# Two relational graph attention layers on one core: tail order, first rounds of the second stage, and three early loads of x

## The chip, the cores and the metric

The kernel runs on one NeuronCore of a Trainium2 chip. The core has a matrix engine (TensorE, PE in the profile, with PEld for its weight loads), VectorE (DVE), ScalarE (ACT), GpSimd (POOL) and SyncE (SP), which work in parallel, each through its own instructions in order, and 16 DMA engines. The metric is the device time of one execution in microseconds, as the median of several runs; lower is better.

## The reference

A graph has 3125 nodes with 768 features each and 53125 edges (25000 random pairs in both directions and one loop per node), sorted by destination. Each edge has one of three relations. Two attention layers of this kind follow each other, then a residual and a layer norm:

```
xr = einsum('nd,rdf->rnf', x, W)              # one dense product per relation
oi, oj = xr[etype, dst], xr[etype, src]
alpha = leaky_relu(oi @ q + oj @ k, 0.2)      # per edge and head
a = softmax of alpha over the edges of one destination
out = segment_sum(a * oj, dst) + b
```

Layer 1 has 4 heads of 192 columns, layer 2 one head of 768. Between the layers stands elu; the result is layernorm(x + layer 2(elu(layer 1(x)))). All in float32.

## The kernel before

The nodes are cut into 25 blocks of 128 (`NB`; the last one has 53 rows), the edges into groups that go with the blocks, each of up to `SL` = 17 slots of 128 edges. Every matmul of the dense products is done on a high and a low part of the operands (`wH`, `wL`), so that three products stand for one. Everything is inside a manual schedule: the order in which Python emits instructions is the order on each engine, and events (`ev`, filled through `when`) say at which step `n` or `k` a function is called. There are four stages, with their times in the profiled execution:

- 0 to 122 us: weights are loaded and split, and products of weights with k and q are made.
- `phase1`, 122 to about 995 us: the dense product of layer 1. A step is one `d_group(n)` (block, relation, half of the columns; `po` L698), six steps per block, some 5.8 us each. `d_row` copies the products out (L713) and stores them as rows of a table in memory (`ftab`). Before a block can be multiplied, `x_load` (L500) reads its rows into `xr`, `d_turn` (L670) transposes them on PE (`px`, L675), and `d_split` (L679) cuts them into parts (ACT L682, DVE L683), adds the bias into `share[4]` (L685) and stores that (L686). `xr` is one buffer. `x_next` at step 6b - 7 loads the next block; for blocks 22 to 24 (`GB` = 21) the turn, split and load stand at m = 1, 3, 5, with m = n - 120. A block of fewer than 128 rows is cleared by a memset (L505) before its load. Between these steps run the attention scores of layer 1: SP loads `T`, `w`, `sT` and `q` per block, POOL gathers `kt` (L462) after DVE's `lim` (L557), and so on. `share` is a list of nine row buffers; 0 to 2 take the rows for the table, others the weights of layer 2 while those are cut (`w_load`, `w_split`).
- `phase2`, about 998 to 2000 us: POOL gathers rows of the table, slot by slot `k`; `high` and `sums` work `LAG` = 5 slots behind. DVE compares destinations with a row of numbers and multiplies by the attention (`selp`, L853); PE uses that as weights and adds the rows up (`acc`, L875). The slots of a block are taken in seven `ROUNDS`, and the sums are issued in two `BATCHES` of rounds. Then `e_y` (L883 to L888: divide, add the bias), `e_x` (exp, L894), `e_h` (L898, L899: elu), `e_t` (transposes, L906), `e_s`, `e_s2` (`hT`, L913, L919), the dense product of layer 2 (L931) and its rows (L939). `last_w2` is a generator; each `next` issues one 1152 KB load (L514) of the last relation's weights of layer 2 on ACT's queue, and the fifth one two DVE copies.
- `phase3`, about 2000 to 2735 us: POOL gathers rows `G` of the second table (44 buffers), about 27.4 us per group. DVE and PE make the softmax (`bc` L1033, `oh` L1059, `a_alpha` L1070 and L1075, transposes L1080, `a_scan` L1086 and L1088, `e` L1091, exp L1095, back L1099, `p` L1104). `high` makes `selp` (L1112), from a pool of 10 buffers of 64 columns, two rounds ahead of `sums` (L1126, `acc`). Then come `e_y` (L1158 to L1162), `e_n` (L1169 to L1173: statistics), `e_sd` (the root, ACT L1177), `e_low` (L1189, L1191) and `e_out` (ACT Identity L1196 and the store). Each store has a manual dependency on the one before; the last one is POOL's scatter L1198.

For each group the events of `phase3` are placed by its first slot; the last groups, which have no gathers left behind them, run one after the other.

Of the kernel before, what the change touches and what calls it, by code (L numbers as in the profile page):

```python
# [8 lines left out]
F32 = mybir.dt.float32  # L9
# [11 lines left out]
P = 128  # L21
# [33 lines left out]
def kernel(  # L55
# [442 lines left out]
        s["q"] = work.tile([P, H1 * R * 3], BF, name="q1", bufs=2)  # L498
        nc.sync.dma_start(s["q"], nodes(b, q1_d))

    def x_load(pre, b):
        n = min(P, N - b * P)
        xs[b] = pre.tile([P, D], F32, name="xr", bufs=1)
        if n < P:
            V.memset(xs[b], 0.0)  # L505
        nc.sync.dma_start(xs[b][:n], x[b * P:b * P + n, :])
# [13 lines left out]
    def phase1(pre, work, psum, wH, wL, qq):  # L520
# [270 lines left out]
        ev[6 * NB - 10].append((lambda b: a_last(), 0))  # L791
        for b in range(2, GB + 1):
            for d, f, o in ((-8, d_turn, 0), (-7, d_split, 0), (-7, x_next, 1)):
                ev.setdefault(6 * b + d, []).append((f, b + o))
        for n in range(max(ev) + 1):
            for f, b in ev.get(n, ()):
                f(b)
            b, i = divmod(n, 6)
            if n == 2:
                nc.sync.dma_start(share[3][:, :D], x[:P, :])  # L800
            if n == 8:
                V.tensor_add(share[4][:, :D], share[3][:, :D], b2r)
                nc.sync.dma_start(xb_d[:P, :], share[4][:, :D])
            m = n - 6 * (GB - 1)
            if m in (1, 3, 5):
                d_turn(GB + 1 + m // 2)
                d_split(GB + 1 + m // 2)
                if m < 5:
                    x_load(pre, GB + 2 + m // 2)
            if m in (9, 17):  # L810
                w2s = second_weights(m // 16, wH, wL)
            if 9 <= m < 25:
                next(w2s, None)
            if 2 <= b < 2 + R * DT:
                if i == 0:
                    w_load(b - 2)
                if i == 2:
                    w_split(b - 2)
            if n < len(groups):
                d_group(n, *groups[n])  # L820
            if 0 < n <= len(groups):
                d_row(*groups[n - 1])


    def phase2(work, psum, wH, wL):
# [31 lines left out]
        def sums(k):  # L857

            b, j = in_turn(k)
            n = [i for i, r in enumerate(rounds(b)) if r[-1] == j]  # L860
            batch = [x for x in BATCHES if n and n[0] == x[-1]]
            if not batch:
                return
            if batch[0][0] == 0:
                blk[b] = {"acc": psum.tile([P, 2, 512], F32, name="acc", bufs=2)}
            acc = blk[b]["acc"]
            o = [(i, t) for r in rounds(b) for i in r for t in WINDOW[i]]
            for m, h in ((m, h) for m in batch[0] for h in range(H1)):
                c = slice(h % 2 * CW, (h % 2 + 1) * CW)
                for i, t in o:  # L870
                    if i not in rounds(b)[m]:
                        continue
                    u = [x for x, y in o if y == t]
                    sel, g = st[b, i]
                    T.matmul(acc[32 * t:32 * t + 32, h // 2, c], sel[:, h, 32 * (t - WINDOW[i][0]):][:, :32],  # L875
                             g[:, h * CW:(h + 1) * CW], start=(i == u[0] and h % 2 == 0), stop=(i == u[-1]),
                             skip_group_check=True)

        def e_y(b):
            s = blk[b]  # L880
            acc = s["acc"][:, :, :HW].rearrange("p c (h f) -> p c h f", h=2)
            rz = work.tile([P, 2, 2], F32, name="rz", bufs=2)
            V.tensor_scalar(rz, acc[:, :, :, F1], EPS, None, op0=ALU.add)  # L883
            V.reciprocal(rz, rz)
            y = s["y"] = work.tile([P, D], F32, name="y", bufs=1)
            for h in range(H1):
                f = slice(h * F1, (h + 1) * F1)
                V.scalar_tensor_tensor(y[:, f], acc[:, h // 2, h % 2, :F1], rz[:, h // 2, h % 2:h % 2 + 1],  # L888
                                       bias1[:, f], op0=ALU.mult, op1=ALU.add)

        def e_x(b):
            s = blk[b]
            s["ey"] = work.tile([P, D], F32, name="ey", bufs=1)
            S.activation(s["ey"], s["y"], AF.Exp)  # L894

        def e_h(b):
            s = blk[b]
# [56 lines left out]

        LAG = 5
        first = SLF + LAG - 1
        for d, f in ((0, e_h), (3, e_t), (3, e_s), (3, e_s2)):
            when(first + d, f, order[0])
        for i, b in enumerate(order):
            e = SLF + i * SL + LAG  # L960
# [11 lines left out]
        for k in range(max(ev) + 1):  # L972
            if k < NK:
                gather(k)
            if k in (14, 19, 23, 26, 28):
                next(last_w2, None)
            if 0 <= k - LAG < NK:
                sums(k - LAG)
            if k == first:
                e_y(order[0])  # L980
                e_x(order[0])
            if 0 <= k - LAG + 2 < NK:
                high(k - LAG + 2)
            for f, a in ev.get(k, []):
                f(*a)
            if k == NK + LAG:
                for b in range(len(xbs)):
                    x_load3(b)
# [6 lines left out]
    def phase3(work, psum):  # L995
# [110 lines left out]
        def high(b, n):  # L1106

            for j in rounds(b)[n]:
                p = blk[b]["p"][:, j:j + 1]
                lo, hi = WINDOW[j][0] * 32, WINDOW[j][-1] * 32 + 32  # L1110
                sel = work.tile([P, 64], F32, name="selp", bufs=10)[:, :hi - lo]
                V.tensor_scalar(sel, row_p[:, lo:hi], dl[:, b, j:j + 1], p, op0=ALU.is_equal, op1=ALU.mult)  # L1112
                st[b, j] = sel

# [96 lines left out]
        def when(k, f, *a):  # L1211
            ev.setdefault(k, []).append((f, a))

        LAG = SL + 10
        for b in range(NB):
            when(max(base(b) - 12, 0), a_load, b)
            q = base(b) - 4 if b > 1 else 2 + 12 * b
            for i in range(5):
                when(q + 2 * i, a_spread, b, i)
                when(q + 1 + 2 * i, a_spread2, b, i)  # L1220
            for d, f in ((10, a_q), (11, a_q2), (12, a_q3)):
                when(q + d, f, b)
            e = base(b) + slots(b)
            for d, f in ((2, a_alpha), (3, a_turn), (4, a_scan), (5, a_exp), (6, a_back), (7, a_put)):
                when(e + d, f, b)
            s = base(b) + LAG + max(slots(b) - SL, -1)
            for n in range(len(ROUNDS)):
                when(s + n - 2, high, b, n)
                when(s + n, sums, b, n)
            s += len(ROUNDS)  # L1230
            if b + len(xbs) < NB:
                when(s + 30, x_load3, b + len(xbs))

            for d, f in ((0, e_y), (1, e_n), (4, e_sd), (5, e_low), (7, e_out)):
                when(s + d + (2 if b == NB - 2 and d > 1 else 0), f, b)
        when(base(NB - 1) + SL, e_ready)
        for k in range(max(ev) + 1):
            if k < NK:
# [591 lines left out]
```

## Time and profile before

| | |
|---|---|
| runs of the kernel | 2748.60, 2750.47, 2752.66 us; median 2750.47 us |
| profiled execution | 2741.27 us |
| its span | 2739.5 us |
| its mean TensorE clock | 0.834 of full speed |
| PE busy | 2054.5 us, 75% of the span |
| DVE busy | 1195.6 us, 44% |
| POOL busy | 1322.5 us, 48% |
| ACT busy | 369.7 us, 13% |

All trace times are from the one profiled execution, counted from the span's start; between it and the median of the runs lie 0.33%. Busy shares are averages over four stages with different limits, so windows of one stage say more than the page's sums. A line of a window holds its start and end, its length, then busy time and count of PE, PEld, DVE, ACT and POOL, the granted clock of TensorE, the busy share of the DMA engines, and GB/s. A line of the chain is: start, length, and what the chain spent it on.

### The profile page before, as it was taken

To read this page: it belongs to the slowest core of one execution; us is meant where nothing else is said; L and a number is where in the kernel's file an instruction comes from. 1 tells how busy PE (TensorE), PEld (TensorE's weight loads), DVE (VectorE), ACT (ScalarE), POOL (GpSimd) and SP (SyncE) were. 2 spreads that over 40 slices of the span, in tenths; PEclk is the share of its full clock that TensorE was granted. 3 is DMA by queue.
4 is the path that set the end of the run, shared out by engine and by line. 5 is a ranking of instruction groups with operands and counts; after the bars stand their busy time and mean duration, and the time that the engine had idled before them with its cause. 6 is when DMAs were issued, how large, how long until landed. Compare 5 with 4: busy or idle time off the path is not lost.

```text
span 2739.5 us, 41906 instructions
## 1 busy us (share of the span) xinstructions
PE 2054.5 (75%) x15027; PEld 1606.6 (59%) x15027; DVE 1195.6 (44%) x4159; ACT 369.7 (13%) x658; POOL 1322.5 (48%) x1326
## 2 busy tenths in 40 slices
PE   7867888777776767888888898889936566565655
PEld 6756676667665645777677777767723232333323
DVE  6423333333332245445544554455424545444444
ACT  5301111111111000101110111111100111111111
POOL 3355555454543454444444434443255656566561
PEclk9967888888887878999999999999966777676777
DMA  7533333333332467666665656665577888877781
GB/s 193 142 95 120 114 114 114 113 106 115 103 108 99 143 213 244 198 201 203 203 200 187 214 185 211 192 212 191 175 271 246 272 267 267 276 253 259 251 262 61
DMA packets 156844, 506.31 MB, mean 185 GB/s; under 512 B 43875, under 2 KB 57069, under 8 KB 156628
## 3 DMA queue, kind: packets, MB, share of 16 engines
q0 software_dynamic: 81904, 331.52, 39.8%
q1 hardware_dynamic: 62926, 156.02, 16.1%
q10 hardware_dynamic: 11798, 16.00, 1.9%
q8 instruction: 122, 2.00, 0.3%
q14 instruction: 94, 0.77, 0.1%
HBM read 412.55 MB, written 95.69 MB: 186 GB/s over the span
## 4 chain that ended last, share of the span: by engine, by line
PE 52%; issue 17%; another core or an unknown queue 12%; DVE 11%; POOL 3%; DMA 3%; ACT 1%; POOLq 0%; ACTq 0%; DVEq 0%; SPq 0%
PE po L931 15%; PE po L698 14%; PE acc L875 9%; PE acc L1126 8%; DVE selp L853 3%; POOL G L462 2%; DMA G<-ftab,ridx 1%; PE bank L285 1%; DVE y L888 1%; PE bc L1033 1%; PE pt L263 1%; PE pt L906 1%; PE po L395 1%; DVE selp L1112 1%
## 5 line engine op out<-in xcount | busy, mean ns | idle before, releaser
L462 POOL DMA_INDIRECT kt<-kt,ridx x374 | 393.6, 1052 | 387.7 <-DVE lim L557 266.3
L698 PE MATMUL po<-wH,xT 128*128 128x384 f32 x1584 | 498.5, 382 | 107.5 <-issue 67.0
L931 PE MATMUL po<-wH,hT 128*128 128x386 f32 (+1 forms) x1800 | 514.7, 361 | 31.7 <-issue 27.3
L462 POOL DMA_INDIRECT G<-ftab,ridx x374 | 372.9, 997 | 242.2 <-PE acc L1126 110.4
L1126 PE MATMUL acc<-G,selp 128*32 128x386 f32 x2488 | 343.2, 621 | 102.6 <-DVE selp L1112 79.9
L698 PEld LDWEIGHTS po<-wH,xT 128*128 128x128 f32 x1584 | 331.2, 215 | 145.0 <-issue 92.0
L931 PEld LDWEIGHTS po<-wH,hT 128*128 128x128 f32 x1800 | 353.0, 202 | 67.3 <-issue 61.9
L853 DVE TENSOR_SCALAR selp<-frow,fdl,pall 128x32 f32<-128x32 f32 (+1 forms) x1688 | 380.3, 309 | 20.1 <-remote 17.3
L462 POOL DMA_INDIRECT share<-ftab,ridx x239 | 238.4, 997 | 299.7 <-PE acc L875 223.4
L931 PE MATMUL po<-wL,hT 128*128 128x386 f32 (+1 forms) x900 | 321.9, 358 | 14.4 <-issue 14.4
L698 PE MATMUL po<-wL,xT 128*128 128x384 f32 x792 | 296.2, 374 | 36.3 <-issue 35.8
L1126 PEld LDWEIGHTS acc<-G,selp 128*32 128x32 f32 x2488 | 190.6, 132 | 217.4 <-DVE selp L1112 107.0
L875 PE MATMUL acc<-share,selp 128*32 128x193 f32 x3208 | 229.6, 335 | 35.0 <-issue 31.4
L462 POOL DMA_INDIRECT g<-ftab,ridx x135 | 134.7, 998 | 191.9 <-PE acc L875 146.5
L698 PEld LDWEIGHTS po<-wL,xT 128*128 128x128 f32 x792 | 170.3, 215 | 48.3 <-issue 48.1
L875 PEld LDWEIGHTS acc<-share,selp 128*32 128x32 f32 x3208 | 131.0, 111 | 107.7 <-issue 77.5
L931 PEld LDWEIGHTS po<-wL,hT 128*128 128x128 f32 x900 | 182.4, 203 | 17.7 <-issue 17.4
L939 ACT COPY r<-po 128x386 f32<-128x386 f32 (+1 forms) x150 | 72.2, 481 | 834.5 <-PE po L931 621.4
L875 PE MATMUL acc<-g,selp 128*32 128x193 f32 x1768 | 139.4, 332 | 18.6 <-issue 15.7
L713 ACT COPY share<-po 128x384 f32<-128x384 f32 x144 | 67.1, 478 | 594.3 <-remote 260.6
L943 DVE COPY q<-po 128x1 f32<-128x1 f32 x75 | 11.6, 155 | 275.8 <-ACT r L939 275.7
L1039 DVE TENSOR_SCALAR sT<-bc,cols 128x512 bf16<-128x512 f32 (+1 forms) x125 | 83.4, 668 | 108.1 <-PE bc L1033 87.4
(245 smaller groups left out, 1986.0 us busy)
## 6 DMA issues: line engine op xcount, KB each, us to landing
ftab<-share SPq DMA_DIRECT2D x75, 386.0 KB
ftab<-r SPq DMA_DIRECT2D x75, 386.0 KB
share<-in_L_gnn_W_dram SPq DMA_DIRECT2D x36, 384.0 KB
w_d<-w2hl SPq DMA_DIRECT2D x18, 768.0 KB
sT<-dr_d SPq DMA_DIRECT2D x25, 544.0 KB
share<-in_x_dram SPq DMA_DIRECT2D x25, 384.0 KB
xb_d<-share SPq DMA_DIRECT2D x25, 384.0 KB
xr<-in_x_dram SPq DMA_DIRECT2D x23, 384.0 KB
```

The source lines that it names most:

```text
L263: T.transpose(pt[:, f, c * P:(c + 1) * P], a[:, (2 * i + f) * P:(2 * i + f + 1) * P], ident)
L285: T.matmul(to, a[:, 2 * i + f, :], t[:, f, :w], start=(n == 0), stop=(n == 2 * DT - 1))
L395: T.matmul(po[g][:, :HALF], a[:, t % 2, :], w[:, r * DT + t, c * HALF:(c + 1) * HALF], start=(t == 0 and n == 0), stop=(t == DT - 1 and n ...
L462: return G.indirect_dma_start(out=to, out_offset=None, in_=tab, in_offset=_index(i[:, j:j + 1]), bounds_check=NP * R - 1, oob_is_err=False)
L698: m = T.matmul(po[:, :HALF], xT[:, s, t, :], w[:, i, sl], start=(n == 0), stop=(n == 3 * DT - 1))
L713: S.copy(to, po[:, :HALF].rearrange("p (h f) -> p h f", h=2))
L853: V.tensor_scalar(sel[:, h, :hi - lo], row[:, lo:hi], dl[:, b, j:j + 1], pall[:, b, j, h:h + 1], op0=ALU.is_equal, op1=ALU.mult)
L875: T.matmul(acc[32 * t:32 * t + 32, h // 2, c], sel[:, h, 32 * (t - WINDOW[i][0]):][:, :32], g[:, h * CW:(h + 1) * CW], start=(i == u[0] an ...
L931: T.matmul(po[:, :wd], hT[:, k, t, :], w[:, r * DT + t, sl], start=(t == 0 and n == 0), stop=(t == DT - 1 and n == 2))
L939: S.copy(o[:, c * HW:c * HW + wd], po[:, :wd])
L1039: V.tensor_scalar(s["sT"][:, 4 * i * P:4 * i * P + n], bc[:, :n], cols[:, b:b + 1], None, op0=ALU.is_equal)
L1126: T.matmul(acc[32 * t:32 * t + 32, c, :HW], st[b, j][:, 32 * (t - WINDOW[j][0]):][:, :32], gs[:, (base(b) + j) % NG, c * HW:(c + 1) * HW], ...
```

## The change

- In `phase1`, block 22 of x is loaded into `share[6]` at m = -8 and block 23 into `share[3]` at m = -3; `share[3]` is last read by a weight split at the step before. Block 24 goes into `xr` at the event that used to load block 22 (n = 119). Turn and split stay at m = 1, 3, 5.
- In `phase2`, the sums of block 0 are called round by round and not in two batches. `e_first` takes the place of `e_y`, `e_x` and `e_h` for block 0: exp is done in two halves, the first as soon as two of the four heads are divided, and elu by halves as well, right after. The first of the five calls of `last_w2` moves from slot 14 to 20 (19, 20, 23, 26, 28 in all).
- In `phase3`, `selp` has two tags, 9 buffers of 32 columns and 8 of 64, which is one group's 17. The sums of group 23 (`NB - 2`) move to `NK` + 4 (rounds 0 and 1) and `NK` + 7 (the rest), NK = 422 being the number of slots, and its `e_*` to `NK` + 14 and on. In the emitted order PE's transposes for the softmax of group 24 (L1080) now stand before the sums of group 23, its back transpose (L1099) between rounds 1 and 2 of these, and the sums of group 24 straight behind. DVE has the 17 selps of group 23, then the softmax of group 24, 15 of its selps, `e_y` of 23, two selps, `e_n` of 23, `e_y` and `e_n` of 24, and only then `e_low` of 23 and of 24.

```diff
--- before.py
+++ after.py
@@ -498,9 +498,9 @@
         s["q"] = work.tile([P, H1 * R * 3], BF, name="q1", bufs=2)
         nc.sync.dma_start(s["q"], nodes(b, q1_d))
 
-    def x_load(pre, b):
+    def x_load(pre, b, to=None):
         n = min(P, N - b * P)
-        xs[b] = pre.tile([P, D], F32, name="xr", bufs=1)
+        xs[b] = pre.tile([P, D], F32, name="xr", bufs=1) if to is None else to[:, :D]
         if n < P:
             V.memset(xs[b], 0.0)
         nc.sync.dma_start(xs[b][:n], x[b * P:b * P + n, :])
@@ -791,7 +791,7 @@
         ev[6 * NB - 10].append((lambda b: a_last(), 0))
         for b in range(2, GB + 1):
             for d, f, o in ((-8, d_turn, 0), (-7, d_split, 0), (-7, x_next, 1)):
-                ev.setdefault(6 * b + d, []).append((f, b + o))
+                ev.setdefault(6 * b + d, []).append((f, NB - 1 if f is x_next and b == GB else b + o))
         for n in range(max(ev) + 1):
             for f, b in ev.get(n, ()):
                 f(b)
@@ -805,8 +805,9 @@
             if m in (1, 3, 5):
                 d_turn(GB + 1 + m // 2)
                 d_split(GB + 1 + m // 2)
-                if m < 5:
-                    x_load(pre, GB + 2 + m // 2)
+
+            if m in (-8, -3):
+                x_load(pre, GB + 1 + (m + 8) // 5, share[6 if m == -8 else 3])
             if m in (9, 17):
                 w2s = second_weights(m // 16, wH, wL)
             if 9 <= m < 25:
@@ -858,7 +859,7 @@
 
             b, j = in_turn(k)
             n = [i for i, r in enumerate(rounds(b)) if r[-1] == j]
-            batch = [x for x in BATCHES if n and n[0] == x[-1]]
+            batch = [x for x in (BATCHES if b else [[m] for m in range(len(ROUNDS))]) if n and n[0] == x[-1]]
             if not batch:
                 return
             if batch[0][0] == 0:
@@ -893,6 +894,27 @@
             s["ey"] = work.tile([P, D], F32, name="ey", bufs=1)
             S.activation(s["ey"], s["y"], AF.Exp)
 
+        def e_first(b):
+
+            s = blk[b]
+            acc = s["acc"][:, :, :HW].rearrange("p c (h f) -> p c h f", h=2)
+            rz = work.tile([P, 2, 2], F32, name="rz", bufs=2)
+            V.tensor_scalar(rz, acc[:, :, :, F1], EPS, None, op0=ALU.add)
+            V.reciprocal(rz, rz)
+            y = work.tile([P, D], F32, name="y", bufs=1)
+            ey = s["ey"] = work.tile([P, D], F32, name="ey", bufs=1)
+            for h in range(H1):
+                f = slice(h * F1, (h + 1) * F1)
+                V.scalar_tensor_tensor(y[:, f], acc[:, h // 2, h % 2, :F1], rz[:, h // 2, h % 2:h % 2 + 1],
+                                       bias1[:, f], op0=ALU.mult, op1=ALU.add)
+                if h % 2:
+                    f = slice(h // 2 * HALF, (h // 2 + 1) * HALF)
+                    S.activation(ey[:, f], y[:, f], AF.Exp)
+            for c in range(2):
+                f = slice(c * HALF, (c + 1) * HALF)
+                V.tensor_scalar(ey[:, f], ey[:, f], 1.0, -1.0, op0=ALU.min, op1=ALU.add)
+                V.scalar_tensor_tensor(ey[:, f], y[:, f], 0.0, ey[:, f], op0=ALU.max, op1=ALU.add)
+
         def e_h(b):
             s = blk[b]
             V.tensor_scalar(s["ey"], s["ey"], 1.0, -1.0, op0=ALU.min, op1=ALU.add)
@@ -954,7 +976,7 @@
 
         LAG = 5
         first = SLF + LAG - 1
-        for d, f in ((0, e_h), (3, e_t), (3, e_s), (3, e_s2)):
+        for d, f in ((3, e_t), (3, e_s), (3, e_s2)):
             when(first + d, f, order[0])
         for i, b in enumerate(order):
             e = SLF + i * SL + LAG
@@ -972,13 +994,12 @@
         for k in range(max(ev) + 1):
             if k < NK:
                 gather(k)
-            if k in (14, 19, 23, 26, 28):
+            if k in (19, 20, 23, 26, 28):
                 next(last_w2, None)
             if 0 <= k - LAG < NK:
                 sums(k - LAG)
             if k == first:
-                e_y(order[0])
-                e_x(order[0])
+                e_first(order[0])
             if 0 <= k - LAG + 2 < NK:
                 high(k - LAG + 2)
             for f, a in ev.get(k, []):
@@ -1108,7 +1129,7 @@
             for j in rounds(b)[n]:
                 p = blk[b]["p"][:, j:j + 1]
                 lo, hi = WINDOW[j][0] * 32, WINDOW[j][-1] * 32 + 32
-                sel = work.tile([P, 64], F32, name="selp", bufs=10)[:, :hi - lo]
+                sel = work.tile([P, hi - lo], F32, name=f"selp{hi - lo}", bufs=9 if hi - lo == 32 else 8)
                 V.tensor_scalar(sel, row_p[:, lo:hi], dl[:, b, j:j + 1], p, op0=ALU.is_equal, op1=ALU.mult)
                 st[b, j] = sel
 
@@ -1226,13 +1247,15 @@
             s = base(b) + LAG + max(slots(b) - SL, -1)
             for n in range(len(ROUNDS)):
                 when(s + n - 2, high, b, n)
-                when(s + n, sums, b, n)
+
+                when(s + n if b != NB - 2 else NK + (4 if n < 2 else 7), sums, b, n)
             s += len(ROUNDS)
             if b + len(xbs) < NB:
                 when(s + 30, x_load3, b + len(xbs))
-
+            if b == NB - 2:
+                s = NK + 14
             for d, f in ((0, e_y), (1, e_n), (4, e_sd), (5, e_low), (7, e_out)):
-                when(s + d + (2 if b == NB - 2 and d > 1 else 0), f, b)
+                when(s + d, f, b)
         when(base(NB - 1) + SL, e_ready)
         for k in range(max(ev) + 1):
             if k < NK:
```

## The prediction

> **What bounds the kernel now.** I read the page's chain and engine parts first, then the windows, and the chain and timeline only where a window stood out.
>
> ```profile
> PE 2054.5 (75%) x15027; PEld 1606.6 (59%) x15027; DVE 1195.6 (44%) x4159; ACT 369.7 (13%) x658; POOL 1322.5 (48%) x1326
> PE 52%; issue 17%; another core or an unknown queue 12%; DVE 11%; POOL 3%; DMA 3%; ACT 1%; POOLq 0%; ACTq 0%; DVEq 0%; SPq 0%
> ```
>
> TensorE is the busiest engine and half of the chain. DMA is 3% of the chain, so one exposed load can only be a place, not a bound. The seven windows of the dense stage that run from one block's kt gathers to the next's show such a place. The columns are PE, PEld, DVE, ACT, POOL, granted clock, DMA share and GB/s:
>
> ```profile
> 705.15:740.36 35.21, 27.39 (x142) 23.67 (x141) 11.79 (x34) 4.61 (x9) 17.84 (x18) 0.81 0.34 111
> 740.36:776.52 36.16, 28.58 (x142) 25.12 (x141) 11.78 (x34) 4.51 (x9) 17.78 (x17) 0.76 0.35 108
> 776.52:811.16 34.64, 25.70 (x142) 22.64 (x141) 11.86 (x34) 4.41 (x9) 17.82 (x17) 0.85 0.35 113
> 811.16:847.12 35.96, 27.21 (x142) 23.89 (x141) 11.84 (x34) 4.41 (x9) 17.82 (x18) 0.81 0.31 98
> 847.12:890.19 43.07, 28.41 (x154) 25.78 (x153) 13.27 (x34) 5.08 (x10) 17.88 (x17) 0.76 0.26 86
> ```
>
> The fifth is 7 to 8 us longer than the others at almost the same PE work. The chain of waits inside it, and the windows around the hole, say why:
>
> ```profile
> 873.99 0.67 DVE xr L505
> 874.72 8.62 DMA xr<-in_x_dram
> 883.47 1.52 PE px L675 x6
> ```
>
> ```profile
> 878.00:883.50 5.50, 0.03 (x1) 0.06 (x1) 0.00 (x0) 0.00 (x0) 0.00 (x0) 0.68 0.06 26
> 883.50:887.00 3.50, 3.50 (x14) 3.50 (x15) 1.14 (x2) 1.18 (x2) 0.00 (x0) 0.53 0.00 2
> 887.00:890.20 3.20, 3.20 (x19) 2.89 (x18) 1.54 (x7) 0.00 (x0) 0.01 (x1) 1.00 0.32 125
> ```
>
> The load of block 24 (53 rows) cannot start until block 23 has been split out of the only xr buffer. It takes 8.62 us, PE stands still for 5.50 us of it, and every engine's row is empty. The 3.5 us after that run at a clock of 0.53, 14 PE records where the next 3.2 us hold 19. The tail (timeline of PE) is the second place:
>
> ```profile
> 2694.51 11.76 PE L1126 MATMUL acc<-G,selp 128*32 128x386 f32 x100
> 2709.98 0.80 PE L1080 MATMUL pa<-fident,al 128*17 128x128 f32 x3 [3.71 <-DVE al L1075]
> 2713.24 0.28 PE L1099 MATMUL pa<-fident,e 17*128 17x17 f32 x1 [2.46 <-ACT e L1095]
> 2715.58 11.47 PE L1126 MATMUL acc<-G,selp 128*32 128x386 f32 x100 [2.05 <-DVE selp L1112]
> ```
>
> PE sums group 23, then waits three times for the softmax of group 24, then sums group 24.
>
> **Part 1, the x loads.** Blocks 22 and 23 are read into two idle row buffers many groups ahead, and block 24 into xr as soon as block 21 is out of it, four dense groups (some 23 us) earlier. The 8.62 us load is then hidden by those groups. What goes is the 5.50 us hole and the slow start after it: 14 records at 3.50/14 = 0.250 us against 3.20/19 = 0.168 us is 1.14 us. Sum 6.6 us. The least is 5.5 (wait alone); the most is 43.07 less the shortest undisturbed window, 34.64, so 8.4. From there to the end every engine's order is fixed and POOL's next gathers wait for DVE's lim (L557), 20.3 us in this window, so the shift is carried on. The moved memset (0.67 us on DVE) lies earlier beside dense work, worth nothing now that no load waits for it. On SP the three loads now stand ahead of the row stores and the loads of T, w, sT and q of later blocks. Those are used four or more groups after they are issued, so 0, and one group's 5.8 us if that cover were gone.
>
> The row on the clock is followed by a page that sizes it otherwise. The Trainium skill, "TensorE: Matmul & The Clock Gate", Part 1, says that after an idle window of about 3.4 us TensorE gets half its clock until about 3.4 us of work have passed; half speed over 3.5 us would be 1.75 us here and the sum 7.3, where the rows give 1.14 and 6.6.
>
> **Part 2, the first block of the second stage.** "Singly" moves nothing on PE: built, PE's order in the first block is what it was, because its DVE comparisons already came round by round; 0. What does change is what follows the sums. Before, in the chain:
>
> ```profile
> 1036.56 1.39 DVE y L888 x4
> 1037.95 0.89 DVE selp L853 x4
> 1038.91 0.57 DVE ey L898
> 1039.50 0.97 DVE ey L899
> 1040.52 1.56 PE pt L906 x6
> ```
>
> Now exp of the first half (half of the 0.84 us of L894, by its length) starts when two y are done, about 1037.3, and the four selp come after. The first half's L898 and L899 (0.29 and 0.49) end near 1038.8, the second's near 1039.7. Three transposes (0.78) run from 1038.9, three from 1039.75, so they end at 1040.5, not 1042.07: 1.6 us (bounds 0.9, the selps alone, and 2.0). The four selps serve later sums, which PE reaches after 6.6 us of dense matmuls.
>
> The first 1152 KB load of wH was issued at 1004.47 among the first gathers; it now goes out at about 1038 with three others. In the 50 us window from 990 the DMA engines were 0.77 busy. PE's sums there run 14 us behind the last gather's landing (1022.45 against 1036.13), so the load's absence need not help: I take 0, with up to 4 us of gain (its 1152 KB at the window's 260 GB/s). The other three loads, issued from 1038.06, landed near 1055, so the fourth lands near 1061, and that relation's weights are first read at 1073; 0 again, up to 2 us for block 1's gathers beside it.
>
> **Part 3, selp buffers.** 17 buffers instead of 10 let DVE finish a group's selps without waiting for PE. Those waits are 39.6 us in 47 places, but they end while PE is working through the very sums that release them, and the steady chain is the ping-pong of bc (L1033), softmax and sums. The 99 queue waits of L1112 at 21 ns are 2 us of DVE. I take 0.5 us of gain, from 4 (a tenth of the waits) to a loss of 1.
>
> **Part 4, the tail.** DVE makes all 17 selps of group 23 (0.24 us each from 2694.14: to 2698.3), then a_alpha(24); from sd to pa took 0.8 us, so pa starts near 2699.2 and ends at 2700.0. Then rounds 0 and 1 of group 23 (32 of 100 records) run under scan, exp and all. PE has stood for almost 5 us, so it starts slowly. Rows for that:
>
> ```profile
> 2715.50:2719.00 3.50, 3.42 (x21) 2.84 (x25) 2.73 (x13) 0.65 (x1) 0.00 (x0) 0.50 0.32 119
> 2719.00:2727.00 8.00, 8.00 (x83) 5.83 (x75) 1.35 (x6) 0.00 (x0) 0.00 (x0) 0.95 0.01 3
> ```
>
> Group 23's own first 3.5 us (2694.5 to 2698.0) hold 23 records, 0.152 each; warm it is about 0.10 (83 in 8.0 us here, in 8.3 us there). So 2.7 us hold 18, 14 more take 1.4: 2704.1; e goes back (0.28) to 2704.4; the other 68 take 6.8 to 2711.2; group 24 follows without a gap, warm, 10.0 to 2721.2 instead of 2727.05. That is 5.9 us, but not all of it reaches the end. ACT's Identity of group 23 waits for its low (L1191), which DVE now does behind all of e_n(24): 2721.2 + 2.94 to sd = 2724.15, low and Identity 1.6 more, 2725.7. Its store takes 3.37 us (row of 2716.18), and POOL's last scatter is ordered behind that landing: 0.38 of queue waits, 0.28 to start: 2729.8 against 2732.02, 2.2 us of gain. Bounds: 2.8 at 0.0964 a record; a loss of 0.3 if all 168 later records cost 0.1147 as before.
>
> **Sum.** 6.6 + 1.6 + 0 + 0.5 + 2.2 = 10.9 us. The profiled execution took 2741.27 us (span 2739.5), so 2730.4; it stood 0.33% under the median of the runs, 2750.47, so the median should come to 2739.6. Worst ends together: 5.5 + 0.9 - 2 - 1 - 0.3 = 3.1 of gain, 2747.4; best ends: 8.4 + 2.0 + 4 + 4 + 2.8 = 21.2, 2729.3. A measurement of this kernel tells about 0.2%, 5.5 us.
>
> **Rivals.**
> (a) Given back. The dense stage's recovered time meets another wait: PE idles 7.6 to 8.9 us in every undisturbed window too (7.2 of it for ACT's share, L713), and the stage's last store gates the first gathers (POOL waits 16.5 us for it). If only 5.5 less 3 us survived, with nothing from steady sums and a tail at its loss end, the gain is 2.5 + 1.6 - 0.3 = 3.8: 2746.7, within 0.2%. Against it: PE's idle in the long window is 14.66 us, 6.4 over the others' mean.
> (b) More. The first block's slow sums are the load's doing, and 4 us come back there with 4 in the steady groups: 10.9 + 4 + 3.5 = 18.4, 2732.1. For it: DMA 0.77 busy. Against: PE trails the landings by 14 us.
> (c) Slower. In the last stage DVE's selps, freed of their waits, move to other moments, beside POOL's gather writing (POOL is busy 327 of 540 us from 2080 to 2620) and PE's reads. If this stretches each of 21 steady groups (27.4 us), at 0.78 us a group (2.8%) it costs 16.4 and the result is 5.5 us slower; that is the point from which it decides. At 0.9: 18.9 - 10.9 = 8.0 slower, 2758.5. For it: DVE waits 112.8 us there on something that the trace does not name. Against: the instructions and their order are the same.
> (d) It does not do what it says: rounds singly are already so on PE, and counted at nothing.
>
> **How the numbers follow.** Forecast 0.64, (a) 0.15, (b) 0.10, (c) 0.11; (d) is inside the forecast. Faster by over 0.2%: forecast and (b), 0.74. Within: 0.15. Slower: 0.11. The range reaches up to (a) and the worst ends, and down close to (b): 2731 to 2749.5.
>
> **What would show it.** Right: the long window at 36 us or less, no DMA wait before px; hT of block 0 about 8 us earlier than 1042 in the span (6.6 + 1.6); one cold stretch in the tail and the last scatter bound by the store of group 23. Wrong: px waiting elsewhere, phase-3 groups that are not 27.4 us, PE waiting on wH near 1066 to 1073, or sums of group 24 still at 11.5 us.

## The result, and the profile after

The changed kernel takes 2743.53 us (median of 12 runs), the kernel before 2751.99 us beside it (12 runs). The ratio is 0.9969, with a 95% interval from 0.9955 to 0.9983: 8.5 us faster. The forecast was 10.9 us less, within a range from 2731 to 2749.5 us.

The two profiled executions differ by half a microsecond only (spans of 2739.0 and 2739.5 us). That is no contradiction: single runs spread over 14 to 19 us, and the page of before had caught a run well under its median. In the trace after, the 102nd row copy of the dense stage (L713), up to which both kernels' work is the same, comes at 712.1 us, before at 707.2 us. So stretches are compared below, each between two marks of one profile, and not times from the start.

The dense stage, windows from one block's kt gathers to the next, as in the prediction:

```profile
710.08:744.86 34.78, 26.79 (x142) 23.75 (x141) 11.79 (x34) 4.53 (x9) 17.80 (x18) 0.80 0.36 112
...
815.28:850.58 35.30, 26.95 (x142) 23.58 (x141) 12.48 (x35) 4.61 (x9) 17.73 (x18) 0.81 0.31 102
850.58:887.43 36.85, 27.66 (x154) 24.21 (x153) 12.64 (x33) 5.08 (x10) 17.86 (x18) 0.81 0.26 85
887.43:923.22 35.79, 27.85 (x136) 23.89 (x135) 7.25 (x27) 3.07 (x7) 17.09 (x17) 0.76 0.51 155
```

The window of 43.07 us takes 36.85. PE's timeline shows block 24's transposes without a wait in front, and warm:

```profile
882.28 0.82 PE L675 MATMUL px<-fident,xr 128*128 128x128 f32 x6
```

The first block of the second stage, on DVE before:

```profile
1036.15 0.16 DVE L883 TENSOR_SCALAR rz<-acc 128x4 f32<-128x4 f32 x1 [13.45 <-remote]
...
1040.38 2.63 DVE L853 TENSOR_SCALAR selp<-frow,fdl,pall 128x32 f32<-128x32 f32 x12
1042.93 0.96 DVE L919 TENSOR_TENSOR hT<-pt,hT 128x768 fp32r<-128x768 f32 x1
```

and after, on DVE and on PE:

```profile
1034.96 0.16 DVE L902 TENSOR_SCALAR rz<-acc 128x4 f32<-128x4 f32 x1 [12.07 <-remote]
...
1038.01 0.56 DVE L916 SCALAR_TENSOR_TENSOR ey<-y,ey 128x384 f32<-128x384 f32 x1
1038.48 3.52 DVE L854 TENSOR_SCALAR selp<-frow,fdl,pall 128x64 f32<-128x64 f32 x16
1041.90 0.97 DVE L941 TENSOR_TENSOR hT<-pt,hT 128x768 fp32r<-128x768 f32 x1
```

```profile
1037.76 1.76 PE L928 MATMUL pt<-fident,ey 128*128 128x128 f32 x6 [7.38 <-DVE ey L915]
...
1042.92 1.01 PE L953 MATMUL po<-wH,hT 128*128 128x386 f32 x2 [1.50 <-DVE hT L941]
```

The transposes start 1.6 us earlier against the last sum, as forecast (2.80 us after DVE's rz, before 4.37). But PE then stops for 1.50 us: hT's low part (L941) stands on DVE behind 16 selps and starts 6.9 us after rz, where before (L919) it stood behind 12 and started 6.8 us after. The tail, on PE, ACT and POOL:

```profile
2701.38 0.80 PE L1101 MATMUL pa<-fident,al 128*17 128x128 f32 x3 [4.80 <-DVE al L1096]
2702.11 5.18 PE L1147 MATMUL acc<-G,selp 128*32 128x386 f32 x32
2707.22 0.23 PE L1120 MATMUL pa<-fident,e 17*128 17x17 f32 x1
2707.39 15.79 PE L1147 MATMUL acc<-G,selp 128*32 128x386 f32 x168
```

```profile
2726.49 1.03 ACT L1217 ACTIVATE pall<-pall,low,sd 128x768 f32<-128x768 f32 x1 [7.58 <-DVE low L1212]
...
2728.04 1.03 ACT L1217 ACTIVATE xb<-xb,low,sd 128x768 f32<-128x768 f32 x1 [0.43 <-DVE low L1212]
```

```profile
2731.53 1.02 POOL L1219 DMA_INDIRECT out_dram<-xb,oidx  x1 [43.27 <-issue]
```

PE's 168 last records run in one piece at 0.094 us each. The scatter starts 2.5 us after the end of ACT's last Identity. Before, it was 0.28 us:

```profile
2730.71 1.03 ACT L1196 ACTIVATE xb<-xb,low,sd 128x768 f32<-128x768 f32 x1 [0.43 <-DVE low L1191]
```

```profile
2732.02 1.02 POOL L1198 DMA_INDIRECT out_dram<-xb,oidx  x1 [45.85 <-ACT xb L1196]
```

It now waits for the store of group 23, as the run "Low of group 23 early" below shows.

### The profile page after: what moved, and what is told of

The parts are those of the page before. It is cut to its first block, busy times and chain, and to the rows that moved or that the text cites. A ratio compares the mean times of both kernels' runs of the same rounds, so it can differ in the third digit from the quotient of the medians.

```text
span 2739.0 us, 41794 instructions
## 1 busy us (share of the span) xinstructions
PE 2068.9 (76%) x15027; PEld 1599.4 (58%) x15027; DVE 1190.7 (43%) x4161; ACT 370.0 (14%) x659; POOL 1322.5 (48%) x1326
## 3 DMA queue, kind: packets, MB, share of 16 engines
q0 software_dynamic: 81904, 331.52, 39.9%
## 5 line engine op out<-in xcount | busy, mean ns | idle before, releaser
L698 PE MATMUL po<-wH,xT 128*128 128x384 f32 x1584 | 508.5, 387 | 102.8 <-issue 77.0
L698 PEld LDWEIGHTS po<-wH,xT 128*128 128x128 f32 x1584 | 335.6, 217 | 141.5 <-issue 105.4
L698 PE MATMUL po<-wL,xT 128*128 128x384 f32 x792 | 300.7, 380 | 45.7 <-issue 45.1
L1147 PEld LDWEIGHTS acc<-G,selp 128*32 128x32 f32 x2488 | 179.2, 131 | 225.9 <-DVE selp L1133 117.2
L698 PEld LDWEIGHTS po<-wL,xT 128*128 128x128 f32 x792 | 172.0, 217 | 62.6 <-issue 62.4
L876 PE MATMUL acc<-g,selp 128*32 128x193 f32 x1768 | 138.8, 329 | 17.4 <-issue 16.7
L713 ACT COPY share<-po 128x384 f32<-128x384 f32 x144 | 67.2, 478 | 595.1 <-issue 207.7
```

The source lines that it names most:

```text
L698: m = T.matmul(po[:, :HALF], xT[:, s, t, :], w[:, i, sl], start=(n == 0), stop=(n == 3 * DT - 1))
L713: S.copy(to, po[:, :HALF].rearrange("p (h f) -> p h f", h=2))
L1147: T.matmul(acc[32 * t:32 * t + 32, c, :HW], st[b, j][:, 32 * (t - WINDOW[j][0]):][:, :32], gs[:, (base(b) + j) % NG, c * HW:(c + 1) * HW], ...
```

## The experiments

The runs fell on several chips, and these are not alike. B, C and D are three different chips; which one A was is not on record. Each comparison is made on one chip. The ratio is taken over all runs and is not the quotient of the two medians beside it.

| comparison | before, us | kernel, us | ratio, 95% interval |
|---|---|---|---|
| chip A: the change | 2751.99 | 2743.53 | 0.9969 (0.9955 to 0.9983) |
| chip B: before again | 2054.07 | 2054.06 | 0.9998 (0.9989 to 1.0007) |
| B: x loads alone | 2054.07 | 2051.07 | 0.9986 (0.9977 to 0.9995) |
| B: first block alone | 2054.07 | 2063.18 | 1.0041 (1.0029 to 1.0054) |
| B: tail alone | 2054.07 | 2059.74 | 1.0023 (1.0014 to 1.0033) |
| chip C: the change again | 2685.4 | 2682.68 | 0.9989 (0.9966 to 1.0013) |
| C: low of group 23 early | 2685.4 | 2673.58 | 0.9956 (0.9933 to 0.9980) |
| C: weight load back at slot 14 | 2685.4 | 2677.75 | 0.9972 (0.9949 to 0.9994) |
| C: x loads, halves, hT early | 2685.4 | 2679.76 | 0.9975 (0.9954 to 0.9997) |
| chip D: x loads alone | 2054.92 | 2052.01 | 0.9992 (0.9982 to 1.0001) |
| D: first block alone | 2054.92 | 2065.72 | 1.0051 (1.0038 to 1.0064) |
| D: tail alone | 2054.92 | 2061.53 | 1.0032 (1.0019 to 1.0045) |
| D: mended | 2054.92 | 2060.33 | 1.0027 (1.0016 to 1.0038) |

On B and D the same program takes 700 us less than on A. What is gone there can be read in the waits of the whole run. On A, before, PE, DVE and POOL:

```profile
PE po L698 <- issue: 119.7, 173, 2.4
...
PE acc L875 <- issue: 47.1, 161, 1.1
```

```profile
DVE oh L1059 <- remote: 151.6, 23, 21.2
...
DVE tq L625 <- remote: 126.7, 21, 16.3
```

```profile
POOL kt L462 <- DVE lim L557: 283.0, 22, 20.3
```

On B, the same kernel, these PE and DVE rows do not exist, and POOL's is this:

```profile
POOL kt L462 <- DVE lim L557: 1.5, 1, 1.5
```

On A and C, PE and DVE stand still in pieces without a cause that the trace names. The two PE rows alone are 167 us. On B and D they do not, so POOL, which writes a gather in 1.0 us everywhere, hardly ever waits for DVE. Idle pieces are not the whole difference: PE is busy for 2054.5 us on A and for 1754.8 us on B with the same instructions, and its granted clock in the dense stage is 0.81 on A (122 to 680 us) and 0.99 on B (122 to 480 us). Why the chips differ was not tried, and stays open. But it gives each part of the change a second test, with another engine as the bound. The reverse is missing: none of the three parts was run alone on A or C, so what each is worth there is read from stretches of the whole change's profiles.

**Before again**

> The kernel before, unchanged, for how much one profile differs from another of the same program. In the changed kernel's profile the dense stage is already 3 to 4 us later than in the profile of before at blocks whose instructions are the same. If that is only the spread between executions, this profile's marks (first kt gathers of each block, first gather of the second stage, exp of each group in the third) differ from those of before by the same 1 to 4 us in both directions; the long window stays at 43 us within 1, the 5.5 us wait for xr stays, the tail from the first selp of group 23 to the last scatter stays at 37.9 us within 0.3. If the shift is the change's doing, the marks agree within 0.5 us. Time: ratio 1.000.

The comparison fell on chip B, so it says nothing on A's 4 us directly. On B the marks of programs with the same instructions differ by 1 to 5 us in both directions all through the dense stage, while from the second block of the second stage to its end the shift between two profiles is constant within 0.2 us. On C four profiles whose dense stages have the same instructions reach the 102nd row copy between 686.3 and 699.3 us. So A's shift ahead of the long window, 4.9 us, is within the spread between executions.

**The x loads alone**, on B and again on D

```diff
-                if m < 5:
-                    x_load(pre, GB + 2 + m // 2)
+            if m in (-8, -3):
+                x_load(pre, GB + 1 + (m + 8) // 5, share[6 if m == -8 else 3])
```

(and block 24 at the event of n = 119, as in the change)

> The three x loads of the change alone. Theory: they carry most of the gain. The window from the kt gathers of one block to the next that took 43.07 us takes 36 to 37, px waits for no DMA; 6.6 us by the forecast, ratio 0.9976, and the tail as before (37.9 us). Rival, given back: the two windows after it get longer by 1 to 1.6 us (34.5 and 34.7 before, 35.8 and 35.4 in the changed kernel), and of the 6.6 only 4 or 5 us are left at the first gather of the second stage: ratio 0.9985.

> The x loads alone once more, with the other parts beside it on one chip. Where the kernel before takes some 2700 us: the last 48 row copies of the dense stage take 281 us instead of 287 (6.2 less in the first comparison), the shift is kept at the first gather of the second stage, ratio 0.9976. Rival, given back as at 2054 us: POOL's kt gathers fill the gap, first gather within 2 us of before against the 102nd row copy; 0.9986 or nearer to 1.

Two stretches from the 102nd row copy show what became of the gain: to the last row copy (PE's side), and to the first gather of the second stage (POOL's side).

| kernel, chip | to the last row copy, us | to the first gather, us |
|---|---|---|
| before, A | 287.1 | 290.7 |
| change, A | 280.9 | 284.5 |
| before, B | 187.7 | 192.2 |
| x loads alone, B | 178.3 | 192.1 |
| x loads alone, D | 178.7 | 192.3 |
| first block alone, D (x loads as before) | 188.2 | 192.7 |

On A both get 6.2 us shorter. That is one pair of profiles, and these stretches spread too: to the first gather, profiles with the same dense stage took 189.1 to 193.5 us on B, and 274.6 to 280.0 us on C. On B and D PE's side gets 9 us shorter (its wait for xr was 9.2 us there) and POOL's side not at all, within that spread. In the profile on D:

```profile
POOL kt L462 <- issue: 124.0, 407, 0.3
```

```profile
PE pa L642 <- DVE al L636: 18.5, 5, 14.0
```

POOL writes its 374 kt gathers back to back, with 0.3 us between them, and the first gather of the second stage has its turn behind them. PE, early now, waits 14.0 us in one place for the attention scores that need the last kt. "Given back" is right on B and D, and the forecast on A. The 1 to 3 us that are left in the times are within or near their intervals.

**The first block alone**, on B and again on D: rounds singly, `e_first`, weight loads at 19, 20, 23, 26 and 28.

> The first block's part alone: rounds singly, exp and elu by halves, the first weight load moved from slot 14 to 20. By the forecast 1.6 us of gain at the transposes and at hT, and it stays. Rival: the transposes come 1.6 us earlier against the last sum, but hT's low part (DVE L941) stands behind 16 selps instead of 12, starts 6.9 us after rz as before (6.8), and PE waits 1.5 us for it between the second and third product: nothing is left at the first dense rows; ratio 1.000. Sums of block 0: 38.2 us from the first gather to rz in both kernels so far, so the absent load gives 0; if the load was the brake, this is 4 us less.

> The first block's part alone once more. Where the kernel before takes some 2700 us: hT's low part 6.9 us after rz as before, PE waits for no weight load, nothing gained or lost: 1.000. Rival: it costs there too (first row copies 1 to 2 us later against rz, as in the first comparison of the changed kernel): 1.0005. At 2054 us: 1.004 again.

On the time both expectations of the first run miss (1.0041); the second's for 2054 us comes near (1.0051). On A the changed kernel's profile has no wait for weights. On D this part costs 10.8 us, and PE's timeline says where:

```profile
758.79 0.41 PE L952 MATMUL po<-wH,hT 128*128 128x384 f32 x1 [2.62 <-DMA wH<-w_d]
...
768.12 0.69 PE L952 MATMUL po<-wL,hT 128*128 128x384 f32 x1 [8.92 <-DMA wL<-w_d]
```

and the chain of waits of that stretch:

```profile
725.71 3.76 ACTq L514
729.46 0.04 issue
729.50 38.57 DMA wL<-w_d
768.07 0.04 issue
768.12 1.97 PE po L952 x5
```

The third and fourth load hold ACT's queue for 4.55 and 7.45 us at the issue, and the last lands 38.6 us after the start of its issue at 729.5 us. On A the fourth holds the queue too, for 3.36 us, but the last bytes of these loads come at 1054.2 us, 14.2 us after the start of that issue. Beside them POOL ran 3 gathers on A in the 17.4 us from the first issue to the last byte, and 26 in 46 us on D. On B PE's waits are 3.6 and 7.0 us. The absent load does help the sums there: from the first gather to rz it takes 23.8 (B) and 23.6 us (D), with the load 25.2 to 27.4 us in the other profiles there (25.9 in the mended kernel, which also takes the rounds singly, so it is the load and not the rounds). On A and C it does not: 38.2 and 38.4 us on A, 36.6 without and 36.5 with the load on C.

**The tail alone**, on B and again on D: the selp tags, the sums of group 23 at `NK` + 4 and `NK` + 7, its `e_*` from `NK` + 14.

> The third stage's part alone: selps in 9 and 8 buffers, sums of group 23 beside the softmax of group 24. Theory: from the first selp of group 23 to the last scatter 35.3 us instead of 37.9 (2.6 less), PE's 168 last records without a gap in 15.8 us, the scatter 2.4 us after ACT's last Identity because it waits for the store of group 23; steady groups as before (27.5 us). Ratio 0.999. Rival: the new buffers lengthen the steady groups (0.1 us each is 2 us in all and takes the tail's gain away); or they shorten them by some tenths.

> The third stage's part alone once more. Where the kernel before takes some 2700 us, POOL has written its last gather 8.8 us before p of group 23, so the softmax of group 24 waits for nothing: from p of group 23 to the last scatter 35.5 us instead of 38.1, ratio 0.999; steady groups as before. At 2054 us the last gather is written 10 us after p, the softmax waits for it, and the span is 42.8 us: 1.002 again. Rival: the sign does not go with the last gather, and the tail is 35.5 on every chip.

On B both expectations miss: the tail is neither 35.3 us nor are the groups before it longer. On D the expectation for 2054 us holds, that the softmax waits for the last gather.

| kernel, chip | p of group 23 to the last scatter, us | POOL's last gather against that p, us |
|---|---|---|
| before, A | 38.1 | -8.8 |
| change, A | 35.5 | -8.8 |
| change, C | 35.7 | -8.8 |
| x loads, halves, hT early (tail as before), C | 37.5 | -8.8 |
| before, B | 37.1 | +11.0 |
| tail alone, B | 42.8 | +9.7 |
| tail alone, D | 43.7 | +11.1 |

The sign goes with the start of the last gather, and on C the new tail is 1.8 us shorter than the old one. On D the softmax of group 24 waits for it on DVE, and PE stands for 13.7 us with the sums of group 23, which used to fill that time, queued behind:

```profile
2020.73 0.19 DVE L1070 TENSOR_TENSOR a<-qe,G 128x17 f32<-128x17 f32 x1 [8.84 <-DMA G<-ftab,ridx]
```

```profile
2021.27 0.80 PE L1080 MATMUL pa<-fident,al 128*17 128x128 f32 x3 [13.73 <-DVE al L1075]
```

The steady groups do not change clear of the spread: from the exp of the second group to that of the 24th 489.7 us before, 491.2 (B) and 490.2 us (D) with this part; on A 613.1 and 612.7, but counted from the third group 586.3 and 588.0.

**The change again**, on C

> The changed kernel itself, because the parts were measured where the kernel before takes 2054 us and not 2752: PE's idle time without a cause (issue) and DVE's unnamed waits (remote) are gone there, and POOL writes gathers without a pause. Theory: the same three edits meet other bounds. At 2054 us before: x loads -3 (POOL's kt gathers take over), first block +8 (PE waits for the moved weight load), tail +5 to +9 (softmax of group 24 waits for the last gathers, with nothing beside it); together some 10 us slower, ratio 1.005. At 2752 us before: 0.997 again. Rival: the parts do not add up, because a block that waits for the weights lets POOL run ahead; then 1.000 to 1.003 at 2054.

C turned out to be like A, slower and with a wider spread. The ratio 0.9989 has 0.9969 inside its interval, and also 1. The sum of the parts at 2054 us was not measured with the whole change.

**Low of group 23 early**, on C

```diff
-                when(s + d, f, b)
+                when(s + (min(d, 2) if b == NB - 2 else d), f, b)
```

> The changed kernel, with the root, low and Identity of group 23 moved ahead of e_y of group 24 on DVE and ACT; PE unchanged. Theory: the last scatter waits for the store of group 23, so its start comes 3.3 us earlier (Identity of 23 ends some 7 us earlier, its store lands before ACT's last Identity is done, and the scatter starts 0.3 us after that Identity and not 2.4): against the changed kernel 0.9985 wherever it runs. Rival: the scatter's 2.4 us are not the store's but POOL's own (five queue waits): then the scatter stays 2.4 us behind the last Identity and nothing is gained.

From p of group 23 to the last scatter it takes 31.9 us instead of 35.7, 3.8 us less. ACT's Identity of group 23 is done 7.5 us ahead of that of 24, and the scatter starts 0.28 us after the last one:

```profile
2656.75 1.03 ACT L1217 ACTIVATE pall<-pall,low,sd 128x768 f32<-128x768 f32 x1 [0.43 <-DVE low L1212]
...
2664.25 1.03 ACT L1217 ACTIVATE xb<-xb,low,sd 128x768 f32<-128x768 f32 x1 [0.43 <-DVE low L1212]
```

```profile
2665.55 1.02 POOL L1219 DMA_INDIRECT out_dram<-xb,oidx  x1 [39.72 <-ACT xb L1217]
```

So the wait was the store's. The time, 9 us under the changed kernel's, moves more than the trace explains; the two intervals overlap.

**The weight load back at slot 14**, on C

```diff
-            if k in (19, 20, 23, 26, 28):
+            if k in (14, 19, 23, 26, 28):
```

> The changed kernel with the first of the last four weight loads back at slot 14. Theory: where PE reaches the third relation of block 0 early (2054 us before), the 10.6 us wait of PE for wH and wL goes and the time is 8 to 12 us under the changed kernel's; where it reaches it late (2752 us before) nothing changes, 0.2 us either way, and the sums of block 0 take as long as without the load. Rival: the load among the first gathers slows them, and block 0's sums take up to 4 us longer, so that half of the gain is lost again.

Nothing changes at the place, as the theory says for a slow chip (36.5 and 36.6 us to rz, no wait for weights in either profile). The 5 us between the medians are inside the intervals.

**x loads and halves, hT ahead of 12 selps, tail as before**, on C (the weight loads, the selp pool and the tail are those of before; the rest of the difference to the changed kernel is this:)

```diff
-        for d, f in ((3, e_t), (3, e_s), (3, e_s2)):
+        for d, f in ((0, e_t), (0, e_s), (0, e_s2)):
```

> The kernel before with only the x loads and the first block's halves, the weight loads as before, and hT's low part (DVE) of block 0 ahead of 12 of the 16 selps. Tail and selp buffers as before. Theory: hT's low part starts 1.5 us earlier against rz than in the changed kernel, PE does not wait for it, and the first dense rows come 1.5 to 3 us earlier; with the x loads 4 to 5 us under the kernel before at 2054 (0.998), 8 to 9 at 2752 (0.997). Rival: POOL's gathers bound the start of the second stage, and whatever PE gains there it waits for rows of block 1: 0.9986, as with the x loads alone.

hT's low part starts 5.5 us after rz instead of 7.0 (6.8 before), and the first dense row is copied 11.9 us after rz instead of 13.0. By the second row copy it is 25.66 against 25.67: the microsecond is gone. So far the rival is right; that POOL's gathers are what takes it back was not shown.

**Mended**, on D: low early, hT early, first load at slot 14.

> The changed kernel with three things mended: low, root and Identity of group 23 ahead of e_y of group 24, hT's low part of block 0 ahead of 12 selps, the first weight load back at slot 14. Theory: x loads 6.2, first block 1, tail 2.6 + 3.5: 13 us under the kernel before where that takes some 2700 us (0.995), and no wait of PE for weights anywhere. At 2054 us: x loads 3, first block 1, tail 4.8 - 2.1 = 2.7 worse: 1 us, 0.9995. Rival: only the tail's parts add up, and the first block's mending is lost in waits for the gathers of block 1: 0.9955, as with the early low alone.

Both expectations miss: 1.0027. The tail is 39.9 us, 2.8 worse than before, as expected. But PE again waits for a weight load:

```profile
760.58 0.69 PE L953 MATMUL po<-wL,hT 128*128 128x384 f32 x1 [5.50 <-DMA wL<-w_d]
```

The earlier hT is the likely cause, but no run separates it. With `e_s` earlier, ACT's queue holds hT's cast ahead of the second load, which goes out at 725.69 us; with the x loads alone it goes out at 722.80, beside exp. The load that PE waits for is the fourth, and that goes out no later (726.70 against 727.29 us), yet its last bytes come at 759.5 us against 752.9. Even with the loads of before the margin on D was thin: there PE turns to these weights at 755.6 us. The sixth row copy comes 45.7 us after rz, with the x loads alone 38.8: 6.8 us, and with the tail's 2.8 that is more than the 5.4 us in the times.

## Why the prediction was right, point by point

**The x loads: right in mechanism on A, and in size as far as one pair of profiles tells.** 6.6 us forecast; the long window is 6.2 us shorter, PE's wait for the load is gone, and from the 102nd row copy to the last one and to the first gather it is 6.2 us too. That this comes so near is in part luck: the stretch spreads by some 5 us between profiles. What was read from A's profile was POOL waiting for DVE's lim, 283 us in all. That is the condition of the forecast: POOL's wait there is 1.5 us in all on B before and 0.5 us on D with the x loads, and the same edit brings PE 9 us and the kernel next to nothing.

**The first block: the step that failed.** The forecast let exp, elu and the transposes set the end of hT. They did move by 1.6 us. But the dense product needs hT's low part as well, and on DVE the four selps taken out from ahead of elu had only moved to a place ahead of L941: 12 selps became 16, and L941 starts 6.9 us after rz where it was 6.8. The sentence that the selps "serve later sums" looked at who reads them and not at what is queued behind them. Nothing was gained. On A the first row copy comes 1.0 us later against rz than before, and the second to sixth some 2.1 us later; but without any edit at this place the first row copy spreads from 11.9 to 13.6 us after rz on B and D, so a loss is not shown either. Nothing was left at the second row copy on C when L941 was moved up. The sign that the prediction named, hT about 8 us earlier, came out near for the high part (ACT's cast, 7.5 us earlier against the 102nd row copy) and short for the low part (L941, 6.0 us).

**The weight load: right on A, for the reason given, and wrong as a rule.** Its bound from the rows, landing near 1061 against a first use at 1073, held on A and C. It was even wide: the matmuls at 1073 still belong to the second relation, and on A the last bytes come at 1054.2 us, while PE turns to the half that needs the third and fourth load 41 us after the first transpose (1037.8 to 1079.1 us). On D it turns to it after 33 us (723.1 to 756.2 us), and the last load takes 38.6 us to land; by PE's waits this is the dearest part of the change there. A margin read where the gathers pause for PE was taken for safe.

**Selp buffers:** 0.5 us forecast; on A the steady groups are 0.4 us shorter by one pair of marks and 1.7 us longer by another, so no gain is shown. The slower rival (c), 16.4 us in longer steady groups, is refuted by the same marks.

**The tail: right.** 2.2 us forecast, 2.6 measured on A (38.1 to 35.5 us), 1.8 on C (37.5 to 35.7). Its steps: pa was put at 2699.2 and stands at 2701.4, in a profile whose first selp of group 23 is 2.1 us later (2696.28 against 2694.14); 32 records were put at 4.1 us and took 5.2; the 168 others were put at 16.8 and took 15.8; the end at the store of group 23, as named. PE's windows from its first matmul after the gap:

```profile
2701.38:2704.88 3.50, 3.50 (x23) 1.25 (x27) 1.90 (x3) 0.31 (x1) 0.00 (x0) 0.50 0.00 0
2704.88:2707.40 2.52, 2.52 (x23) 0.55 (x13) 0.00 (x0) 0.00 (x0) 0.00 (x0) 0.59 0.00 0
2707.40:2723.20 15.80, 15.78 (x169) 6.16 (x168) 7.16 (x25) 1.49 (x2) 0.00 (x0) 1.00 0.01 3
```

The clock stays at half for 5.6 us (2701.38 to 2706.97), not 3.5, and then is full to the end of the sums; on D, with the tail alone, it changes 3.4 us after PE's first matmul (2021.27 to 2024.66). The cold stretch is the term of this part that was put too short. So the 32 records take 5.2 us here and 4.1 us on D. The Trainium skill, "TensorE: Matmul & The Clock Gate", Part 1, says that the window of some 3.4 us runs freely, so that the place of the change varies, by about half a microsecond. That it varies agrees; the size does not, with 2.2 us between these two profiles.

**The sum.** The time fell by 8.5 us, with an interval from 4.7 to 12.4. The forecast's 10.9 lies inside it, so that the first block's 1.6 us and the selps' 0.5 are missing is a reading of the traces, not of the times. The pieces of the two profiles do not add up to 8.5 either: after the 102nd row copy the change is 6.2 us shorter to the first gather, 3.5 us longer from there to p of group 23 (2.4 of it in the second stage), and 2.6 us shorter in the tail, together 5.4 us. On C the middle stretch spreads by 4.7 us between profiles of the changed kernel with and without the first weight load at slot 14, so whether the 3.5 us are the change's doing stays open. Rival (a), given back, is what happens on B and D to the x loads; rival (b), a first block freed by the absent load, is refuted on A (38.2 and 38.4 us to rz) and worth some 2 us on B and D.

## What to carry to other kernels

When an instruction is moved out of the way of one consumer, read on in its engine's queue: whatever stands behind its new place is now late, and it counts as much as who reads its result. A load that is hidden with a margin of some microseconds on one chip need not be on another, where the consumer comes earlier and more gathers run beside the load. So issue loads early and not just in time, and look at what is ahead of them in the queue that issues them. Before filling a gap with later work, ask what the gap's own work was covering: the sums of group 23 covered the last gathers where these came late.

## What the runs showed of the hardware

The same program took 2752 us on A, 2685 on C, 2054 on B and 2055 on D. On A and C PE and DVE show idle pieces that the trace gives no cause for (119.7 us ahead of PE's line L698 on A), on B and D there are none at these lines, while POOL's gathers take 1.0 us each everywhere. So the same edit was worth -8.5 us in one comparison, and its parts, each alone, -3, +9 and +6 us in another. Four loads of 1152 KB issued within 8 us held ACT's queue at the issue itself, for 3.36 us on A and for 4.55 and 7.45 us on D, and the last landed after 14.2 us on A and 38.6 us on D. The clock of PE went from half to full 3.4 us after its first matmul in D's tail and 5.6 us after it in A's.
